# A transformer block with cross attention: residual rows, layer norm statistics and stores moved, and one more pair of softmax units transposed on the vector engine

## The chip, the cores and the metric

One core of a Trainium2 chip runs the kernel. The core has a matrix engine (TensorE, PE in the profile, with its weight loads as PEld), a vector engine (VectorE, DVE), an activation engine (ScalarE, ACT), a general engine (GpSimd, POOL) and a sync engine (SyncE, SP) that here only issues transfers. Each engine works through its own instructions in order, and waits on semaphores for what other engines or transfers still owe it. Transfers (DMA) can be issued by SP, ACT or POOL; an instruction that issues one and has to wait holds up everything behind it on that engine.

The metric is the time of one execution in microseconds. The runs before had a median of 835.01 us (834.54 to 835.21). The profile comes from one further execution.

## What is computed

Four batches (B = 4) of 512 rows of width 512, all in float32. With `x` the rows and `c` the context rows of a batch, the reference is, cut to what matters:

```
h   = layer_norm(x, ln1_w, ln1_b)
q   = heads(h @ q_w + q_b);  k = heads(c @ k_w + k_b);  v = heads(c @ v_w + v_b)     # 16 heads of 32
a   = softmax(q k^T / sqrt(32) + mask) v
hid = a @ cproj_w + cproj_b + x
y   = gelu(layer_norm(hid, ln2_w, ln2_b) @ fc_w + fc_b) @ proj_w + proj_b            # inner width 2048
out = hid + y
```

## The kernel before

**Tiling.** The program is a straight line of instructions that Python loops write out. The 16 heads of a batch are handled in four groups of four; a group of a batch is `w` (0 to 15, batch = w // 4). The 512 query rows of a group go in four *units* of 128 rows; unit `u = 4 w + qt` counts from 0 to 63. Two neighbouring units are a *pair*, `2 w + half`, 0 to 31.

**A unit** (`scores`, L227). TensorE makes the scores of four heads into a PSUM tile `sc`, of which there is only one, so the next unit's scores wait until VectorE has read it. VectorE adds the mask and takes the row minimum of the negated scores (L239, four instructions); ScalarE makes the exponentials and their sums (L243, four).

**Turning a unit** (`turn`, L247). The probabilities have to be transposed before they meet `v`. In most pairs VectorE transposes 32 by 32 blocks into a tile `tb` (L271, four per unit; after the second unit also the reciprocal sums, L276 to L279), and 16 transfers of 136 KB, issued by SP, exchange the blocks between the partition groups (`copies`, L299). There are two `tb` tiles, so pair p + 2 (or the next one after it to use them) waits for the exchange of pair p. The exchange writes to a tile `pT`, of which there is one, or, for the pairs in `IN_G`, to `gt`, a tile that the MLP needs only later; the pairs in `IN_XE` use `xe` at the end. `exchange` (L288) keeps back a pair bound for `pT` until the pair before it in `pT` has been attended. The pairs in `ON_PE` are instead transposed on TensorE (L257, 16 small matrix instructions a unit into PSUM), copied out by VectorE and ScalarE (L260, L262), and their sums transposed on TensorE as well (`turn_sums`, L326).

**Attending a pair** (`attend`, L336): TensorE multiplies by `v` (L356), VectorE scales the result into `oT` (L361). It comes ahead of the scores of a later unit; by default pair p is attended at unit 2 p + 4, and the table `AT` sets other units.

**Work between the units.** The lists `first[w]` and `later[w]` (L757 to L827) hold what is put between the units of a group: projections to k, q and v of a group two or more ahead (`prep_k`, `prep_q`, `prep_v`), layer norm 1 of a later batch (`inputs`: loads of x into four `xn` tiles, statistics, normalisation, transposes on TensorE with eviction by VectorE and ScalarE), the projection `cproj` of a finished batch (`C`), layer norm 2, and the pieces of the MLP of batches 0 and 1 (`fc`, `proj`). Each piece has a cost (3.4 for a chain of matrix work, 0.5 for a transpose step, 0 for loads and vector work); the loop at L830 hands pieces out so that each half of a unit gets its share of the list's cost. So a piece's place in the list sets its place on every engine's queue.

**Loads.** `Q[0]` issues most loads: POOL in batch 0 (w = 0 to 3), SP from w = 4 on (L833). `load_w` loads a group's weights, `load_mlp` keeps up to eight tiles of MLP weights ahead, `load_hid` loads residual rows into `hid` and adds a bias row to them on POOL (`add_row`, L368). For batch 0 the residual rows are x itself; for the later batches `cproj` adds x and the bias (tiles `ct`), stores the sum to a DRAM tile `xa` (L401), and `load_yn` and `load_hid` read it back.

**cproj and layer norm 2** (L389, L414). `cproj` of row tile t is one chain of TensorE, then VectorE adds it to `hid` (batch 0) or `ct` (L397). In batches 0 and 3 VectorE takes the statistics of the sum at once (`ln_stat`, two instructions). `ln_rs` makes the reciprocal deviations on POOL, `norm2` normalises on VectorE, `ln2_turn` transposes on TensorE into `yT`.

**The end.** The MLPs of batches 2 and 3 run after the attention (`last_mlps`, L513), with a scheme of seven products in place of eight. It works in pairs of inner tiles (`fc_pair`), and VectorE makes the sums that it needs, of the weights (`sum_wa`), of `yT` (`y_sums`) and of the results.

Of the kernel before, what the change touches and what calls it, by code (L numbers as in the profile page):

```python
# [40 lines left out]
P = 128  # L44
B, L, D, H = 4, 512, 512, 16
HD = D // H
INNER = 4 * D
NT = L // P
# [8 lines left out]
AHEAD = 3  # L57
NORMAL = 2
LAG = 4
IN_G = (2, 5, 7)  # L60
IN_XE = (29, 31)
AT = {7: 1, 9: 2, 13: 4, 15: 5}
ON_PE = (0, 3)
MW = 8
WARM = 14
PW = 2 * NT * HG * HD
# [7 lines left out]
def xattn_block(ctx: ExitStack, tc: tile.TileContext, x, encT, mask, q_w, k_w, v_w, c_w, fc_w, p_w, vecs, rows, out):  # L74
# [29 lines left out]
    S = {}  # L104
# [6 lines left out]
    def ln_stat(key, t, src):  # L111
        if t == 0:
            S["mv", key] = small.tile([P, NT, 2], F32, tag="mv", name=f"mv{key[0]}_{key[1]}")
        st = small.tile([P, 6], F32, tag="st", name=f"st{key[0]}_{key[1]}_{t}")
        nc.vector.bn_stats(st, src)
        nc.vector.bn_aggr(S["mv", key][:, t, :], st)
# [63 lines left out]
    def load_w(w, queue=None, names=("wk", "wq", "wv")):  # L180

        if w >= NW:
            return
        g = w % NG
        for n, src in (("wk", k_w), ("wq", q_w), ("wv", v_w)):
            if n in names:
                S[n, w] = (two if n == "wk" else one).tile([P, ND, P], F32, tag=n, name=f"{n}_{w}")
                (queue or Q[0]).dma_start(out=S[n, w], in_=src[:, g, :, :])
# [21 lines left out]
    def prep_v(w):  # L210
        b = w // NG
        v = five.tile([P, NT, P], F32, tag="v", name=f"v_{w}")
        acc = acc_tile(f"accv_{w}")
        for t in range(NT):
            for d in range(ND):
                nc.tensor.matmul(  # L216
                    acc[:, ts(t, P)], eT[:, d, ts(t, P)], S["wv", w][:, d, :],
                    start=(d == 0), stop=(d == ND - 1),
                )
        load_w(w + 1, names=("wv",))  # L220
        nc.scalar.copy(v, acc.rearrange("p (t f) -> p t f", t=NT))  # L221
        bias = row[:, 2, ts(w % NG, P)]
        nc.gpsimd.tensor_tensor(v, v, bias[:, None, :].broadcast_to([P, NT, P]), ALU.add)  # L223
        S["v", w] = v
# [151 lines left out]
        for t in ts_:  # L376
            add_row(S["hid", b, t], 1 if b else 0)

    def load_ct(b, t):

        if t == 0:
            S["xa", b] = dram.tile([L, D], F32, tag=f"xa{b}", name=f"xa{b}")
        if b == B - 1:
            S["ct", b, t] = tiles.tile([P, D], F32, tag="xn", name=f"ct_{b}_{t}")
        else:
            S["ct", b, t] = two.tile([P, D], F32, tag="ct", name=f"ct_{b}_{t}")
        Q[0].dma_start(out=S["ct", b, t], in_=x[b, ts(t, P), :])

    def cproj(b, t):  # L389
        h = S["hid", b, t] if b == 0 else S["ct", b, t]  # L390
        if b:
            for i in range(NT if b == B - 1 else 2) if t == 0 else (t,) if t > 1 and b < B - 1 else ():
                add_row(S["ct", b, i], 0)
        acc = acc_tile(f"accc_{b}_{t}")
        for g in range(NG):
            nc.tensor.matmul(acc, S["oT", b][:, g, ts(t, P)], wc[:, g, :], start=(g == 0), stop=(g == NG - 1))  # L396
        nc.vector.tensor_tensor(h, acc, h, ALU.add)  # L397
        if b in (0, B - 1):
            ln_stat((2, b), t, h)
        if b:  # L400
            nc.sync.dma_start(out=S["xa", b][ts(t, P), :], in_=h)  # L401
            if t + 2 < NT and b < B - 1:
                load_ct(b, t + 2)

    def load_yn(b):

# [2 lines left out]
            Q[0].dma_start(out=S["yn", b][t], in_=S["xa", b][ts(t, P), :])  # L409

    def stat2(b, t):
        ln_stat((2, b), t, S["yn", b][t])

    def norm2(b, t):  # L414
        if b == 0 and t == 0:
            S["yn", b] = [tiles.tile([P, D], F32, tag="xn", name=f"xn2_{b}_{i}") for i in range(NT)]
        if b == B - 1 and t == 0:
            S["yn", b] = [S["ct", b, i] for i in range(NT)]
        ln_norm((2, b), t, S["yn", b][t], S["yn", b][t] if b else S["hid", b, t])
# [42 lines left out]
    def proj(b, q, t):  # L462
        acc = acc_tile(f"accp_{b}_{q}_{t}")
        for k in range(FQ):
            nc.tensor.matmul(  # L465
                acc, gT[q % 2][:, k, ts(t, P)], S["pw", b, q * FQ + k], start=(k == 0), stop=(k == FQ - 1)
            )
        h = S["hid", b, t]
        nc.vector.tensor_tensor(h, acc, h, ALU.add)  # L469
        if q == NQ - 1:  # L470
            nc.sync.dma_start(out=out[b, ts(t, P), :], in_=h)
        count[1] += 1
        load_mlp()

# [38 lines left out]
    def last_mlps():  # L513
# [137 lines left out]
        for b in range(NORMAL, B):  # L651
            for c in range(NP):
                if b == NORMAL:
                    for i in range(2):
                        nc.sync.dma_start(out=pb[:, c, i, :], in_=p_w[ts(2 * c + i, P), :])
                fc_pair(b, c, lambda: sum_wa(c + 1) if c + 1 < NP else None)
                if c + 2 < NP:
                    load_wa(c + 2)
                elif b + 1 < B:
                    load_wa(c + 2 - NP)  # L660
                if c % 2 == 0 and c:
                    g_sums(c - 2)
                if b + 1 < B and 1 <= c <= NT:
                    norm2(b + 1, c - 1)
            g_sums(NP - 2)

            def sums(b=b):
                if b == NORMAL:
                    for c in range(0, NP, 2):
                        p_sums(c)  # L670
                if b + 1 < B:
                    load_hid(b + 1, range(NT))

            def turns(b=b):
                if b + 1 < B:
                    run(turns2(b + 1))

            def middle(b=b):
                if b + 1 < B:
                    y_sums(b + 1)  # L680
                    sum_wa(0)

            project(b, sums, turns, middle)
# [5 lines left out]
    def do(fn):  # L689
        return [(0.0, fn)]  # L690
# [69 lines left out]
    load2, k2, q2, v2 = A(2)  # L760
    load3, k3, q3, v3 = A(3)
    load4, k4, q4, v4 = A(4)
    first[0] = do(lambda: load_w(2, names=("wk",))) + [(CHAIN, lambda: prep_v(1)), (CHAIN, lambda: prep_q(1))] + x1 + [load2, k2, q2]
    first[1] = x2[:1] + [v2, load3, k3] + x2[1:2] + [q3] + x2[2:] + [v3] + x4 + x3
    first[2] = do(load_mlp) + [load4, q4, k4, v4] + A(5)[:2]
    first[3] = A(5)[2:] + A(6)
    mlp = []
    for p in range(NORMAL):
# [6 lines left out]
    def hid_(b, *ts_):  # L775
        return do(lambda: load_hid(b, ts_))
# [7 lines left out]
    def rs(b):  # L784
        return do(lambda: ln_rs((2, b)))
# [6 lines left out]


    x1, x2, x3, x4 = inputs(2)
    first[3] += x1
    load, k, q, v = A(7)
    c, t2 = C(0), turns2(0)
    first[4] = [load, k] + x2[:2] + [q] + x2[2:] + [v] + x3[:2] + x4 + hid_(0, 0, 1, 2, 3)
    later[4] = c[:1] + x3[2:] + c[1:] + rs(0)
    load, k, q, v = A(8)  # L800
    first[5] = norm(0, 0, 1) + [load, q] + norm(0, 2, 3) + [k] + t2 + [v] + do(lambda: proj_bias(0)) + some(5)
    load, k, q, v = A(9)
    x1, x2, x3, x4 = inputs(3)
    first[6] = [load, k, q] + some(5) + [v] + x1
# [65 lines left out]
    load_wa(1)  # L870
    sum_wa(0)
    run(C(B - 1))
    ln_rs((2, B - 1))
    load_hid(NORMAL, range(NT))
    att.close()
    last_mlps()
# [44 lines left out]
```

## Time and profile before

| what | value |
|---|---|
| median of the runs | 835.01 us |
| profiled execution, its own time | 838.42 us |
| span in that execution | 836.6 us |
| TensorE busy | 812.7 us, 4064 matrix instructions |
| VectorE busy | 557.9 us |
| ScalarE busy | 342.3 us |
| GpSimd busy | 109.5 us |
| transfers | 136.87 MB, mean 164 GB/s |

How to read the profile. The busy part of the page gives each engine's time; a row of digits shows it in 40 slices of the span, in tenths, and PEclk is the clock that TensorE was granted, in tenths of full speed. A line of a timeline has start, duration, engine, line of the kernel, operation, the tiles written and read, the shape and a count; where the engine sat idle before it, square brackets hold the idle time and what ended it. SPq and POOL lines with DMA_DIRECT2D are issues of transfers. A line of waits has the engine and line that waited, whom for, the total, the number of times and the longest. A line of the table by stages has the stretch, its length, and then each engine's busy time with its number of instructions (PE, PEld, DVE, ACT, POOL), the granted clock, the share of the transfer engines and GB/s. A piece of the chain has start, duration and what ran. A matrix instruction of the program is two in the profile, so x32 in a row of `av` is one attended pair.

### The profile page before, as it was taken

What the parts mean: (1) busy time and instruction counts of PE and PEld (TensorE: products, weight loads), DVE (VectorE), ACT (ScalarE), POOL (GpSimd) and SP (SyncE); (2) the same over time, 40 slices, a digit from 0 to 9 for tenths busy, and PEclk for the clock granted to TensorE, in tenths of its full rate; (3) what the DMA queues carried; (4) which work ended last, traced back from release to release, by engine and by line L of the source; (5) the groups of instructions that cost most, each with busy time, mean ns of one, the idle gap of its engine ahead of it and who ended that gap; (6) DMA issues with size and microseconds to landing.
All of it is one profiled execution on the core that took longest, in us unless ns stands there. A gap on an engine that the chain in (4) does not pass through costs nothing.

```text
span 836.6 us, 11984 instructions
## 1 busy us (share of the span) xinstructions
PE 812.7 (97%) x4064; PEld 472.9 (57%) x4064; DVE 557.9 (67%) x1259; ACT 342.3 (41%) x740; POOL 109.5 (13%) x132
## 2 busy tenths in 40 slices
PE   9998999979999999999999999999999999999998
PEld 6545545434445554453554435444446888888887
DVE  3596988478666785876887486877337987268511
ACT  2555654316765553455544357455200431023200
POOL 2313312023000021000100210000013003200011
PEclk9998999989999999999999999999999999999999
DMA  5465798828777777687777776985835550022001
GB/s 205 157 154 158 231 236 223 204 75 197 185 184 209 208 202 217 172 211 186 211 202 194 222 200 166 247 196 126 247 108 182 160 193 34 15 87 76 12 13 38
DMA packets 59164, 136.87 MB, mean 164 GB/s; under 512 B 12144, under 2 KB 14320, under 8 KB 58976
## 3 DMA queue, kind: packets, MB, share of 16 engines
q1 hardware_dynamic: 55056, 122.99, 54.5%
q0 software_dynamic: 3520, 12.00, 4.5%
q10 hardware_dynamic: 528, 1.14, 0.6%
q8 instruction: 32, 0.52, 0.3%
q14 instruction: 28, 0.23, 0.1%
HBM read 61.89 MB, written 7.34 MB: 83 GB/s over the span
## 4 chain that ended last, share of the span: by engine, by line
PE 82%; DVE 7%; DMA 4%; SPq 3%; POOL 1%; issue 1%; ACT 0%; DVEq 0%; ACTq 0%; POOLq 0%
PE accp L465 13%; PE accf L455 12%; PE q L559 12%; PE sc L234 7%; PE av L356 6%; PE accv L216 5%; PE accq L204 5%; PE acck L195 5%; PE accc L396 3%; DVE s L239 2%; SPq L313 2%; DVE tb L271 2%; DMA xn<-x_dram 2%; PE q4p L599 2%; PE q3p L599 2%; PE q5p L599 2%
## 5 line engine op out<-in xcount | busy, mean ns | idle before, releaser
L243 ACT ACTIVATE s<-s,mn 128x512 f32<-128x512 f32 x256 | 181.6, 710 | 181.5 <-DVE mn L239 181.2
L239 DVE CUSTOM_DVE_ANT_0 s<-sc,mb 128x512 f32<-128x512 f32 x256 | 161.2, 686 | 47.9 <-PE sc L234 47.8
L271 DVE STREAM_TRANSPOSE tb<-s 128x512 f32<-128x512 f32 x240 | 152.6, 684 | 6.1 <-ACT s L243 5.0
L455 PE MATMUL accf<-yT,fcw 128*128 128x512 f32 x256 | 114.9, 599 | 0.0
L465 PE MATMUL accp<-pw,gt 128*128 128x512 f32 x256 | 114.3, 598 | 0.0
L455 PEld LDWEIGHTS accf<-yT,fcw 128*128 128x128 f32 x256 | 47.1, 190 | 65.0 <-issue 61.0
L465 PEld LDWEIGHTS accp<-pw,gt 128*128 128x128 f32 x256 | 47.4, 190 | 63.2 <-issue 60.5
L234 PE MATMUL sc<-kT,qT 32*128 32x512 f32 x512 | 73.6, 645 | 2.2 <-DVE mn L239 1.4
L396 PE MATMUL accc<-wc,oT 128*128 128x512 f32 x128 | 59.2, 614 | 6.7 <-DVE hid L397 6.7
L216 PEld LDWEIGHTS accv<-wv,xe 128*128 128x128 f32 x512 | 58.9, 192 | 9.4 <-issue 8.4
L559 PE MATMUL q<-ys,gt 128*128 128x256 f32 x256 | 60.3, 380 | 0.7 <-issue 0.7
L216 PE MATMUL accv<-wv,xe 128*128 128x128 f32 x512 | 60.6, 277 | 0.0
L195 PE MATMUL acck<-xe,wk 128*128 128x512 f32 x128 | 58.7, 601 | 0.0
L204 PE MATMUL accq<-xe,wq 128*128 128x512 f32 x128 | 58.5, 599 | 0.0
L356 PE MATMUL av<-pT,v 128*32 128x256 f32 x864 | 53.9, 391 | 4.5 <-DMA pT<-tb 3.2
L559 PEld LDWEIGHTS q<-ys,gt 128*128 128x128 f32 x256 | 48.5, 190 | 7.9 <-issue 1.0
L469 DVE TENSOR_TENSOR hid<-accp,hid 128x512 f32<-128x512 f32 x32 | 21.9, 684 | 40.2 <-PE accp L465 40.1
L243 ACT ACTIVATION_READ_ACCUMULATOR s<-s,mn 128x1 f32 x256 | 47.7, 187 | 0.0
L223 POOL TENSOR_TENSOR v<-v,row 128x512 f32<-128x512 f32 x16 | 20.4, 1276 | 203.4 <-ACT v L221 203.2
L396 PEld LDWEIGHTS accc<-wc,oT 128*128 128x128 f32 x128 | 24.4, 196 | 39.5 <-issue 31.0
L559 PE MATMUL q<-yT,gt 128*128 128x256 f32 x192 | 46.3, 379 | 0.0
L356 PEld LDWEIGHTS av<-pT,v 128*32 128x32 f32 x864 | 26.5, 112 | 33.9 <-issue 18.7
(122 smaller groups left out, 875.6 us busy)
## 6 DMA issues: line engine op xcount, KB each, us to landing
pT<-tb SPq DMA_DIRECT2D x400, 136.0 KB, 2.4
pw<-p_w_dram SPq DMA_DIRECT2D x32, 256.0 KB, 4.0
gt<-fc_w_dram SPq DMA_DIRECT2D x32, 256.0 KB, 2.9
gt<-tb SPq DMA_DIRECT2D x48, 136.0 KB, 3.8
fcw<-fc_w_dram SPq DMA_DIRECT2D x24, 256.0 KB, 3.3
pb<-p_w_dram SPq DMA_DIRECT2D x16, 256.0 KB, 3.7
xe<-tb SPq DMA_DIRECT2D x24, 136.0 KB, 2.4
xe<-encT_dram SPq DMA_DIRECT2D x12, 256.0 KB, 3.8
```

What stands on the lines that cost most here:

```text
L195: nc.tensor.matmul(acc, S["wk", w][:, d, :], eT[:, d, :], start=(d == 0), stop=(d == ND - 1))
L204: nc.tensor.matmul(acc, S["wq", w][:, d, :], xT[:, d, :], start=(d == 0), stop=(d == ND - 1))
L216: nc.tensor.matmul(acc[:, ts(t, P)], eT[:, d, ts(t, P)], S["wv", w][:, d, :], start=(d == 0), stop=(d == ND - 1),)
L234: nc.tensor.matmul(sc[:, h, :], qT[r, ts(qt, P)], kT[r, :], start=True, stop=True)
L239: nc.vector.tensor_tensor_reduce(out=s, in0=sc[:, h, :], in1=S["mb", w // NG], scale=1.0, scalar=FMAX, op0=ALU.add, op1=ALU.min, accum_out=mn,
L243: nc.scalar.activation(s, s, AF.Exp, bias=mn, scale=-1.0, accum_out=sums[:, qt, h : h + 1])
L271: nc.vector.transpose(tv[:, q, h], S["ps", w, qt][h])
L356: nc.tensor.matmul(av[ts(h, HD), : 2 * P].rearrange(shape, **kw), v[:, t, ts(h, HD)], p[t][h], start=(t == 0), stop=(t == NT - 1),)
L396: nc.tensor.matmul(acc, S["oT", b][:, g, ts(t, P)], wc[:, g, :], start=(g == 0), stop=(g == NG - 1))
L455: nc.tensor.matmul(acc, S["fcw", b, f][:, d, :], S["yT", b][:, d, :], start=(d == 0), stop=(d == ND - 1))
L465: nc.tensor.matmul(acc, gT[q % 2][:, k, ts(t, P)], S["pw", b, q * FQ + k], start=(k == 0), stop=(k == FQ - 1))
L559: nc.tensor.matmul(o, a[:, k], y[:, k], start=(k == 0), stop=(k == 1))
```

## The change

- `IN_G` becomes (2, 4, 6) and `ON_PE` becomes (0,). Pair 3 is now turned by VectorE and exchanged like the others. The pairs of batch 0 from 1 on use `pT` and `gt` by turns.
- `AT` attends pair 3 at unit 11 (10 before) and pair 6 at unit 17 (16 before).
- The first eight MLP weight tiles are loaded at the end of `first[0]` instead of the start of `first[2]`, in both places by POOL.
- The residual rows of batch 0 are loaded at the end of `first[3]`, ahead of x for batch 2, by POOL, where they were at the end of `first[4]`, by SP. Their row additions on POOL move along.
- Batch 0's statistics for layer norm 2 leave `cproj` and stand in `first[5]`, after unit 20's scores; its normalisation follows, and its transposes come after v's projection instead of before.
- Batch 3's statistics leave `cproj` and stand between the inner pairs 0, 1 and 3 of batch 2's last MLP; its normalisation moves from pairs 1 to 4 to pairs 4, 5 and 7.
- In batches 1 and 2 the stores to `xa` and the loads of `ct` for t = 2 and 3 are issued by POOL instead of SP; so are the four output stores of batch 0.

```diff
-IN_G = (2, 5, 7)
+IN_G = (2, 4, 6)
-AT = {7: 1, 9: 2, 13: 4, 15: 5}
-ON_PE = (0, 3)
+AT = {7: 1, 9: 2, 11: 3, 13: 4, 15: 5, 17: 6}
+ON_PE = (0,)
...
-    def load_ct(b, t):
+    def load_ct(b, t, queue=None):
...
-        Q[0].dma_start(out=S["ct", b, t], in_=x[b, ts(t, P), :])
+        (queue or Q[0]).dma_start(out=S["ct", b, t], in_=x[b, ts(t, P), :])
...
         nc.vector.tensor_tensor(h, acc, h, ALU.add)
-        if b in (0, B - 1):
-            ln_stat((2, b), t, h)
         if b:
-            nc.sync.dma_start(out=S["xa", b][ts(t, P), :], in_=h)
+            (nc.sync if b == B - 1 else nc.gpsimd).dma_start(out=S["xa", b][ts(t, P), :], in_=h)
             if t + 2 < NT and b < B - 1:
-                load_ct(b, t + 2)
+                load_ct(b, t + 2, nc.gpsimd)
...
-        ln_stat((2, b), t, S["yn", b][t])
+        ln_stat((2, b), t, S["hid", b, t] if b == 0 else S["ct", b, t] if b == B - 1 else S["yn", b][t])
...
-            nc.sync.dma_start(out=out[b, ts(t, P), :], in_=h)
+            (nc.gpsimd if b == 0 else nc.sync).dma_start(out=out[b, ts(t, P), :], in_=h)
...
-                if b + 1 < B and 1 <= c <= NT:
-                    norm2(b + 1, c - 1)
+
+                if b + 1 < B:
+                    for t in {0: (0,), 1: (1, 2), 3: (3,)}.get(c, ()):
+                        stat2(b + 1, t)
+                    if c == 3:
+                        ln_rs((2, b + 1))
+                    for t in {4: (0,), 5: (1, 2), 7: (3,)}.get(c, ()):
+                        norm2(b + 1, t)
...
-    first[0] = do(lambda: load_w(2, names=("wk",))) + [(CHAIN, lambda: prep_v(1)), (CHAIN, lambda: prep_q(1))] + x1 + [load2, k2, q2]
+    first[0] = do(lambda: load_w(2, names=("wk",))) + [(CHAIN, lambda: prep_v(1)), (CHAIN, lambda: prep_q(1))] + x1 + [load2, k2, q2] + do(load_mlp)
...
-    first[2] = do(load_mlp) + [load4, q4, k4, v4] + A(5)[:2]
+    first[2] = [load4, q4, k4, v4] + A(5)[:2]
...
-    first[3] += x1
+    first[3] += hid_(0, 0, 1, 2, 3) + x1
...
-    first[4] = [load, k] + x2[:2] + [q] + x2[2:] + [v] + x3[:2] + x4 + hid_(0, 0, 1, 2, 3)
-    later[4] = c[:1] + x3[2:] + c[1:] + rs(0)
+    first[4] = [load, k] + x2[:2] + [q] + x2[2:] + [v] + x3[:2] + x4
+    later[4] = c[:1] + x3[2:] + c[1:]
...
-    first[5] = norm(0, 0, 1) + [load, q] + norm(0, 2, 3) + [k] + t2 + [v] + do(lambda: proj_bias(0)) + some(5)
+    first[5] = stat(0, 0, 1) + [load, q] + stat(0, 2, 3) + rs(0) + [k] + norm(0, 0, 1, 2, 3) + [v]
+    first[5] += t2 + do(lambda: proj_bias(0)) + some(5)
...
     run(C(B - 1))
-    ln_rs((2, B - 1))
```

## The prediction

> **What bounds the kernel now.** I read the page's engine shares first, then TensorE's waits, then the timelines of the places that these waits name.
>
> ```profile
> PE 812.7 (97%) x4064; PEld 472.9 (57%) x4064; DVE 557.9 (67%) x1259; ACT 342.3 (41%) x740; POOL 109.5 (13%) x132
> PEclk9998999989999999999999999999999999999999
> ```
>
> TensorE has 812.7 of 836.6 us, so an edit is worth what it takes out of TensorE's work, of its idle stretches, or of the two slices with a lower clock. Its waits, and where they lie:
>
> ```profile
> PE accc L396 <- DVE hid L397: 6.7, 1, 6.7
> PE av L356 <- DMA pT<-tb: 3.2, 2, 1.7
> PE tp L136 <- DVE xn L127: 1.7, 1, 1.7
> PE tpp L257 <- ACT s L243: 1.6, 1, 1.6
> ...
> 65.72 2.16 PE L257 MATMUL tpp<-ident,s 128*128 128x128 f32 x12 [1.60 <-ACT s L243]
> ...
> 172.88 5.63 PE L396 MATMUL accc<-wc,oT 128*128 128x512 f32 x8 [6.70 <-DVE hid L397]
> ...
> 498.69 1.93 PE L356 MATMUL av<-pT,v 128*32 128x256 f32 x32 [1.67 <-DMA pT<-tb]
> ```
>
> Nearly all of it stands before 200 us; 498.69 is in batch 2. VectorE is the second bound there:
>
> ```profile
> 49.13:135.80 86.67, 81.18 (x566) 45.77 (x562) 71.93 (x179) 46.59 (x116) 22.25 (x35) 0.96 0.77 207
> ```
>
> Units 4 to 16 hold 81.2 us of TensorE and 71.9 of VectorE. Last, the queues around the long wait:
>
> ```profile
> 132.74 0.55 POOL L188 DMA_DIRECT2D wv<-v_w_dram  x1 [6.15 <-PE accv L216]
> 133.30 1.28 POOL L223 TENSOR_TENSOR v<-v,row 128x512 f32<-128x512 f32 x1
> 134.51 2.21 POOL L154 DMA_DIRECT2D xn<-x_dram  x4
> ...
> 135.29 13.09 SPq L313 DMA_DIRECT2D gt<-tb  x16
> ...
> 166.36 1.85 SPq L375 DMA_DIRECT2D hid<-x_dram  x4
> ...
> 170.84 4.93 POOL L368 TENSOR_TENSOR hid<-hid,row 128x512 f32<-128x512 f32 x4 [19.96 <-DMA hid<-x_dram]
> ```
>
> The rows of x for the first residual (hid) are issued at 166.36, behind pair 8's 16 exchange transfers on SP; VectorE and TensorE wait for them.
>
> **Pair 3 leaves TensorE.** Two unit transposes at 1.75 us (the chain's piece at 29.52) and the sums' 0.31 go: 3.8 us of TensorE, with its waits of 1.60 and 0.53 for unit 6's exponentials. VectorE gains eight tb transposes (24.2 us for 40, so 0.61 each) and one of 0.45, and loses four copies of 0.69: +2.5. Then VectorE needs 74.4 us in this stage, and TensorE 81.2 - 3.8 - 2.9 (what the half-clock stretch at 67 to 74 us cost: av 3.57 for 1.86, the scores after it 1.72 for 1.07, the rest in tpp) = 74.5. Neither covers the other any more, so I walk it. Pair 3's exchange costs SP 16 x 0.64 = 10.2 us and lands about 2.4 later; its turn ends near 78, SP is free from about 75, attend(3) comes near 95: hidden.
>
> The eight fc loads (2.1 MB) move from 83 us to right behind the wq load at 47.42 on POOL, 8 x 0.55 = 4.4 us, in front of the next weight load at 54.34, so nothing queues. But they meet pair 1's exchange, which SP issues from 49.6 and which landed at 63.9 (my reading of the transfers' own landings); 2.1 MB at 353 GB/s (79 to 95 us moved 247 GB/s at a transfer share of 0.70) is 6 us of transfer, of which 2 to 3 fit ahead of the exchange. I put the landing at 67 (bounds 64 to 70). attend(1), freed of the transposes, wants it at 64.1: a wait of 3 takes the place of 2.1. The projection of q behind layer norm 1's transposes then waits for VectorE, which reaches those evictions at 78.4 to 80, against 83.1 before. From there my walk stays 3.3 to 5 us ahead to unit 13: **g = 4.0**. Attend(6), behind two projections now, loses its wait for the exchange: **+1.5**.
>
> On the clock the Trainium skill ("TensorE: Matmul & The Clock Gate", What's actually happening) says that it halves after an idle window of some 3.4 us. This trace dropped it after 1.6 us of idle with transposes around it, and did not after 1.67 us at 497. By the page my 3 us wait at 64 costs nothing more, by the row up to 2.9; g lies between.
>
> **hid moves to the end of w = 3, ahead of x for batch 2.** It takes away the 6.70, the half-clock that followed (5.63 for 3.6: 2.0), and VectorE's backlog from it: 0.48 before scores, 1.67 and three of 0.13 in layer norm 2's transposes. **+11.2.** But on POOL these are four loads (2.2 us) and then four row additions (1.27 each), which wait for the landings, and only then the four xn loads. Before, xn was issued at 134.51 to 136.18 beside an exchange and landed 3.0 to 8.2 us later:
>
> ```profile
> 136.18 8.20 DMA xn<-x_dram
> ```
>
> Let E be the end of v's projection of w = 6 (132.44 before). hid takes xn's old place: it lands at E+5 to E+12, the fourth addition ends at E+13.2, the xn loads go out at E+13.2 to E+15.4, at the tail of pair 7's exchange and beside three weight loads. With 4 to 5 us each the last lands at E+19.5 (bounds: without collision in hid E+16.5; with another 8.2, E+23). VectorE stands at its statistics, before unit 17's minima; then 0.85 + 0.42 + 2.46 + 0.46 until the first transpose: E+23.7. TensorE reaches it at E + 1.07 + 3.6 + 3.63 + 1.86 + 1.07 + 3.67 = E+14.9. **-8.8**, nothing else being queued ahead of it, and a half clock behind it: none to 2.2, I take **-1.1**.
>
> **Layer norm 2 of batch 0.** Statistics (4 x 0.8) now stand behind unit 20's minima, and the transposes directly ahead of fc(0), with v's projection before them, no longer between. From scores(20) to fc(0) VectorE has 2.5 minima, 3.3 statistics, 2.4 tb, 1.8 norm, 2.5 minima, 0.7 eviction, 2.4 tb, 0.95 sums, 0.7 eviction = 17.3; TensorE has 7.2 + 1.1 + 3.6 + 1.8 = 13.7. **-3.6** (cover gone; before, the 3.6 of v hid the evictions).
>
> Up to fc(0): 4.0 + 1.5 + 11.2 - 8.8 - 1.1 - 3.6 = +3.2. After it TensorE is bound again, VectorE with slack.
>
> **xa stores, ct loads and batch 0's outputs to POOL.** In batch 2:
>
> ```profile
> 473.85 0.53 SPq L401 DMA_DIRECT2D xa<-ct  x1
> 476.36 0.34 SPq L387 DMA_DIRECT2D ct<-x_dram  x1
> ...
> 481.74 4.59 SPq L401 DMA_DIRECT2D xa<-ct  x2
> 486.47 10.25 SPq L313 DMA_DIRECT2D pT<-tb  x16
> ```
>
> The first store waits for SP, and the last store's wait for VectorE holds the next exchange from 485.4 to 486.47. On POOL, 12 issues of 0.55 per two batches besides waits; queued behind are ct's additions (about 0.8 us earlier than before by my walk) and v's, which have a unit's slack. The exchange goes out 1.0 to 1.9 us earlier and the waits of 1.67 and 0.29 (scores at 488.82) end: **+1.7** (0.5 to 2.0). Batch 1 has 0.2 to win.
>
> Against it stands a rule of the skill ("SBUF — State Buffer", A bandwidth-pool intuition that's wrong): a transfer issued by POOL can be starved by VectorE's two-port operations, 3.1 us for 0.62. The POOL rows above took 0.55 with VectorE over 85% busy, so I cost an issue at 0.55.
>
> **Batch 3's statistics.**
>
> ```profile
> 639.12 0.69 DVE L487 TENSOR_TENSOR ys<-yT,ys 128x512 f32<-128x512 f32 x1
> ...
> 639.91 3.69 PE L559 MATMUL q<-ys,gt 128*128 128x256 f32 x16 [0.67 <-issue]
> ```
>
> Without the 0.87 of statistics ahead of them the ys sums end before TensorE asks: **+0.7**. The 3.4 us go into a stage with 42.8 of 46 us busy on VectorE, but its results are read a pair (5.8 us) later, and at most 1.7 comes at once: hidden.
>
> **Sum.** 3.2 + 1.7 + 0.2 + 0.7 = 5.8. The profiled execution took 838.42 with a span of 836.6; its span falls to about 830.8. The median of the runs, 835.01, is 3.4 below that execution; I take the difference off it: 829.2. A change under 0.2% (1.7 us) can't be told from none.
>
> **Rivals.**
> - *hid's landings don't collide* (0.22): xn at E+16.5 and no half clock: 3 + 1.1 more, 825. For it: hid before landed in 4.4 to 4.9. Against: pair 7's exchange is on SP in just those microseconds.
> - *The front gains nothing* (0.14): pair 1 lands at 70 with a half clock behind (g = 2) and xn comes at E+22: -4.5, some 833.8. That the front part doesn't do what it is for is this case.
> - *POOL is starved* (0.07), the slower end: if the issues of hid and xn behind v(6) take the page's 3.1 us, 8 x 2.55 = 20 us later xn, about 849. It decides from 5.8 + 1.7 = 7.5 us of delay, 1.5 us an issue.
> - The sum as it stands (0.57): 826.5 to 832.5.
>
> Range: from 823.5 (first rival with 1.5 below) to 835 (second with 1.2 above). Faster: 0.57 + 0.22 and a third of the second, 0.83; same 0.09; slower 0.08.
>
> **What would show it.** In the trace after: no tpp in unit 6, and av for pair 1 waiting 0 to 6 us for its exchange; no wait of accc for hid; instead layer norm 1's second set of transposes waiting 6 to 12 us for xn; fc(0) waiting 2 to 5 us on an eviction; no wait for an exchange at 490 to 500; ys without wait. I am wrong if xn lands before E+15, if VectorE's stage from unit 4 to 16 takes over 83 us, or if POOL's issues grow.

## The result, and the profile after

The changed kernel is slower. Its median is 841.15 us (839.38 to 845.05), beside 835.72 us (834.54 to 839.2) of the kernel before on the same chip, six runs each (those of before include the three whose median is 835.01): 5.4 us between the medians. The ratio on record, which is not the quotient of the medians (1.0065), is 1.0055, 95% interval 1.0031 to 1.0078, about 4.6 us. In a second comparison, on the chip of several of the experiments below, it was 840.42 against 837.19: ratio 1.0032 (1.0017 to 1.0047), 2.7 us. The forecast was 829.2 with a range of 823.5 to 835. The profiled execution took 841.57 us with a span of 839.8, beside 838.42 and 836.6 before.

Engine shares and granted clock of the page after:

```profile
PE 809.9 (96%) x4030; PEld 469.5 (56%) x4030; DVE 557.1 (66%) x1264; ACT 339.9 (40%) x735; POOL 119.8 (14%) x152
PEclk9998899699999999999999999999999999999999
```

TensorE is busy 2.8 us less, as pair 3's transposes are gone, and yet the span is 3.2 longer. The clock row shows why to look ahead of 170 us: slices of 8, 8 and 6 tenths, where before there were two of 8. TensorE's waits after:

```profile
PE tp L137 <- ACT s L244: 10.2, 1, 10.2
PE av L357 <- DMA gt<-tb: 8.9, 2, 5.7
PE sc L235 <- DVE mn L240: 2.4, 2, 1.8
PE av L357 <- ACT gt L455: 1.7, 1, 1.7
...
PE tp L137 <- ACT v L222: 0.9, 1, 0.9
...
PE accf L454 <- DVE yT L140: 0.4, 1, 0.4
```

The wait for hid (6.70) is gone, as are the waits in unit 6's transposes. In their place stand one wait of 10.17 and two of 5.66 and 3.20. TensorE's timeline gives their places:

```profile
68.59 3.64 PE L357 MATMUL av<-pT,v 128*32 128x256 f32 x32 [5.66 <-DMA gt<-tb]
...
99.00 3.64 PE L357 MATMUL av<-pT,v 128*32 128x256 f32 x32 [3.20 <-DMA gt<-tb]
...
159.59 2.60 PE L137 MATMUL tp<-ident,xn 128*128 128x128 f32 x8 [10.17 <-ACT s L244]
162.12 3.64 PE L357 MATMUL av<-pT,v 128*32 128x256 f32 x32
...
493.30 1.14 PE L235 MATMUL sc<-kT,qT 32*128 32x512 f32 x8 [1.80 <-DVE mn L240]
...
643.62 3.62 PE L558 MATMUL q<-ys,gt 128*128 128x256 f32 x16
```

The first two are waits for the exchanges of pair 1 and pair 3. The profile names the transfer that ended last, here one of the next pair (`gt`); by their own landings pair 1's last transfer came at 68.21 and pair 3's at 98.65. The third is for the normalized rows of batch 2, whose last load lands at 155.30 (below); the profile names the last engine of the chain from there. The fourth is for batch 2's row 2. An attended pair takes 1.93 us at full clock and 3.64 behind each of the first three waits: the granted clock was half there. The last line is the `ys` product of batch 3, which now waits for nothing. The issues of transfers that explain the first three, on SP and on POOL:

```profile
46.76 4.31 POOL L446 DMA_DIRECT2D fcw<-fc_w_dram  x8
...
48.47 15.26 SPq L314 DMA_DIRECT2D pT<-tb  x16
...
80.80 13.97 SPq L314 DMA_DIRECT2D pT<-tb  x16
...
136.64 2.21 POOL L376 DMA_DIRECT2D hid<-x_dram  x4
139.63 2.67 POOL L369 TENSOR_TENSOR hid<-hid,row 128x512 f32<-128x512 f32 x2 [0.78 <-DMA hid<-x_dram]
143.27 1.28 POOL L369 TENSOR_TENSOR hid<-hid,row 128x512 f32<-128x512 f32 x1 [0.96 <-DMA hid<-x_dram]
145.41 1.27 POOL L369 TENSOR_TENSOR hid<-hid,row 128x512 f32<-128x512 f32 x1 [0.87 <-DMA hid<-x_dram]
146.63 2.18 POOL L155 DMA_DIRECT2D xn<-x_dram  x4
```

The eight fc loads go out just ahead of pair 1's exchange, whose 16 issues then take 15.26 us instead of the 10.47 of before. Pair 3's take 13.97. The rows of x for batch 2 (`xn`) go out only at 146.63, when the fourth addition to hid is done; their last transfer runs in the chain of work from 148.26 to 155.30:

```profile
148.26 7.04 DMA xn<-x_dram
```

Where the time went is read from the start of each unit's scores, in the kernel's profile less in that of before, with the difference at unit 0 taken off (microseconds; minus is sooner). The last column is the end of the span. The labels are those of the experiments below.

| kernel | unit 15 | unit 22 | unit 52 | unit 54 | end |
|---|---|---|---|---|---|
| after | +3.33 | +4.44 | +4.17 | +5.74 | +4.35 |
| forecast for it | -4.0 | -3.2 | -3.4 | -5.1 | -5.8 |
| after, second profile | +2.63 | +3.81 | +3.54 | +6.57 | +5.18 |
| e1_stores_sp | -0.88 | +0.83 | +0.56 | -0.14 | -1.52 |
| e3_x_first | +0.09 | -2.58 | -2.85 | +1.15 | -0.24 |
| e2_pair3_pe | -0.38 | +1.98 | +1.71 | +0.26 | -1.14 |
| e4b_fc_late | -4.49 | -1.81 | -2.08 | -0.17 | -1.55 |
| e12_hid_behind | +1.78 | -8.52 | -8.59 | -4.29 | -5.44 |
| e10_hid_early | -4.69 | -14.38 | -14.65 | -16.08 | -16.79 |
| e9_b_front | +3.65 | -8.58 | -7.31 | -9.14 | -9.16 |
| e11_front_fc_late | -4.50 | -13.43 | -12.62 | -12.99 | -13.01 |
| e5_b_hid_early | -2.24 | -13.54 | -13.50 | -13.59 | -13.59 |
| e6_b_stats3 | -2.44 | +0.56 | +0.80 | -0.51 | -1.65 |
| e8_b_stores_pool | -2.18 | -0.43 | -0.70 | -2.09 | -2.24 |
| v1 | -4.61 | -15.75 | -16.02 | -17.00 | -18.15 |
| v2_pool | -4.23 | -15.96 | -16.23 | -17.73 | -19.11 |

Against the forecast 7.3 us are missing by unit 15, and 3.3 more between units 52 and 54. The stretch between 15 and 22, with the longest wait of all, came out as summed (1.1 lost, 0.8 forecast).

One profiled execution is not the kernel, though. Up to unit 15 five of these executions run the same program as the changed kernel (its own two, e1, e3 and e12), and they stand at +3.33, +2.63, -0.88, +0.09 and +1.78. All five wait 5.6 to 8.5 us for pair 1; what sets them apart is in good part whether the wait for pair 3 (2.17 to 3.20 us) is followed by half clock, as in the first two, or not. So by unit 15 the miss is 3.1 to 7.3 us. Of the old order (before, e5, e6, e8) the same column has 0, -2.24, -2.44 and -2.18.

### The profile page after: what moved, and what is told of

Read it like the earlier page. It is cut to its first block, busy times and chain, and to the rows that moved or that the text cites. A ratio compares the mean times of both kernels' runs of the same rounds, so it can differ in the third digit from the quotient of the medians.

```text
span 839.8 us, 11953 instructions
## 1 busy us (share of the span) xinstructions
PE 809.9 (96%) x4030; PEld 469.5 (56%) x4030; DVE 557.1 (66%) x1264; ACT 339.9 (40%) x735; POOL 119.8 (14%) x152
## 3 DMA queue, kind: packets, MB, share of 16 engines
q10 hardware_dynamic: 528, 1.14, 0.6%
## 4 chain that ended last, share of the span: by engine, by line
PE 85%; DMA 7%; DVE 3%; ACT 2%; POOL 1%; issue 1%; SPq 1%; DVEq 0%; POOLq 0%; ACTq 0%
PE accp L464 13%; PE accf L454 12%; PE q L558 12%; PE sc L235 7%; PE av L357 7%; PE accv L217 6%; PE acck L196 5%; PE accc L397 5%; PE accq L205 5%; DMA pT<-tb 3%; PE tp L137 2%; PE q4p L598 2%; PE q3p L598 2%; PE q5p L598 2%; PE q6p L598 2%; PE q1p L598 2%
## 5 line engine op out<-in xcount | busy, mean ns | idle before, releaser
L272 DVE STREAM_TRANSPOSE tb<-s 128x512 f32<-128x512 f32 x248 | 157.6, 683 | 12.1 <-DMA gt<-tb 6.8
L357 PE MATMUL av<-pT,v 128*32 128x256 f32 x864 | 57.3, 410 | 10.6 <-DMA gt<-tb 8.9
L397 PE MATMUL accc<-wc,oT 128*128 128x512 f32 x128 | 57.0, 597 | 0.0
L235 PEld LDWEIGHTS sc<-kT,qT 32*128 32x128 f32 x512 | 20.6, 188 | 39.1 <-issue 20.4
```

Of the source, the lines that this page charges most:

```text
L235: nc.tensor.matmul(sc[:, h, :], qT[r, ts(qt, P)], kT[r, :], start=True, stop=True)
L272: nc.vector.transpose(tv[:, q, h], S["ps", w, qt][h])
L357: nc.tensor.matmul(av[ts(h, HD), : 2 * P].rearrange(shape, **kw), v[:, t, ts(h, HD)], p[t][h], start=(t == 0), stop=(t == NT - 1),)
```

## The experiments

Every comparison is against the kernel before, run beside it on the same chip (four chips, with medians of before of 837.36, 837.19, 836.92 and 836.59 us). Theory at the start: the front lost its gain to the fc loads, which meet pair 1's exchange, and batch 2 its gain to the order on POOL. Rival: the loss belongs to pair 3, whose exchange was costed at nothing.

**Undoing one part of the changed kernel.** First its stores, back on SP (statistics, rows of hid and everything else as changed):

```diff
-            (nc.sync if b == B - 1 else nc.gpsimd).dma_start(out=S["xa", b]...)
+            nc.sync.dma_start(out=S["xa", b]...)
...
-                load_ct(b, t + 2, nc.gpsimd)
+                load_ct(b, t + 2)
...
-            (nc.gpsimd if b == 0 else nc.sync).dma_start(out=out[b, ...])
+            nc.sync.dma_start(out=out[b, ...])
```

> The changed kernel with one part undone: xa stores, the later ct loads and batch 0's outputs are issued by SP again. Theory (POOL's order costs time in batch 2: the addition of ct_2 stands behind the issue of ct_3's load, which waits for the landing of a store): the waits at units 53 and 54, 1.80 and 1.74 us in the changed kernel, return to the 0.29 and 1.67 of before, 1.5 us faster than the changed kernel, some 839.7 us against its 841.2. Rival (the stores' place does not matter, the wait at 53 comes from the front part's shift): same time as the changed kernel within 0.5 us, and the two waits stay.

Measured: 837.12, ratio 1.0003 (0.9982 to 1.0024). In its profile units 52 to 54 gain 0.7 where the changed kernel lost 1.6: 2.3 us, where the theory had 1.5. But unit 15 was also 4.2 us sooner than in the changed kernel's profile, where this edit does nothing: the wait for pair 3's exchange was 2.17 in this execution, not 3.20, and no half clock followed. By the ratios the edit is worth 2.4 to 4.4 us; its own stretch accounts for 2.3.

Then pair 3, back on TensorE, with its attends and exchanges (fc loads stay early, attend(6) late):

```diff
-IN_G = (2, 4, 6)
...
-AT = {7: 1, 9: 2, 11: 3, 13: 4, 15: 5, 17: 6}
-ON_PE = (0,)
+IN_G = (2, 5, 7)
...
+AT = {7: 1, 9: 2, 13: 4, 15: 5, 17: 6}
+ON_PE = (0, 3)
```

> The changed kernel with pair 3 transposed on TensorE again (pair 6 still attended at unit 17, all else as changed). Theory (the seventh exchange is what the front can't hold: it runs beside the context loads, lands 18 us after its start, and TensorE waits 3.20 us and then runs at half clock): unit 11's scores come where they were before, within 1 us, instead of 3.6 us later, with no wait for an exchange at pair 3; pair 1's wait of 5.66 shrinks below 2 because the transposes of unit 6 lie in it; all in all 2.5 to 4 us faster than the changed kernel, 837 to 838.7. Rival (pair 1's collision with the fc loads is what costs, pair 3 only takes its place): less than 1 us faster, the wait for pair 1 stays above 4.

Measured: 836.4, ratio 0.9998 (0.9985 to 1.0011), 0.6 us below the theory's band, and by the ratios 2.8 to 4.8 us below the changed kernel; unit 12 starts within 0.4 us of before. Pair 1's exchange is stretched here too:

```profile
49.08 15.93 SPq L314 DMA_DIRECT2D pT<-tb  x16
...
70.88 1.93 PE L357 MATMUL av<-pT,v 128*32 128x256 f32 x32 [2.39 <-ACT pT L263]
```

but the pair waits 2.39 us and not 5.66, since pair 3's transposes stand ahead of it, and full clock follows. (The copy that the line names writes into the `tb` tile that pair 1's exchange frees at 70.2.) So the early fc loads cost less while that cover is there, none against the profile of before and some 2 us at unit 15 against the executions of the old order without its half clock (e5, e6): most of the loss comes from the two edits together.

Now the fc loads alone, put to the front of `first[5]`, behind pair 9's exchange:

```diff
-    first[0] = ... + [load2, k2, q2] + do(load_mlp)
+    first[0] = ... + [load2, k2, q2]
...
-    first[5] = stat(0, 0, 1) + [load, q] + ...
+    first[5] = do(load_mlp) + stat(0, 0, 1) + [load, q] + ...
```

> The changed kernel with the first eight fc loads issued only at the start of w = 5, by SP, so that they meet neither pair 1's nor pair 3's exchange. Theory (the collision costs pair 1's wait): attend(1) waits under 2 us instead of 5.66 and no half clock follows, so unit 8 comes 4 us earlier; pair 3's wait stays between 1 and 3 us since the context loads still collide with it; fc(0) then waits for its weights not at all or up to 2 us, and 3 to 5 us are left: 836 to 838. Rival (VectorE bound the stage from unit 4 to 16 anyway, 74.4 us of work): unit 13 comes less than 2 us earlier than in the changed kernel.

Measured: 835.47, ratio 0.9964 (0.9948 to 0.998), 0.5 us below its band and by the ratios 5.7 to 7.6 us below the changed kernel. Pair 1's 16 issues take 10.47 us again:

```profile
48.83 10.47 SPq L314 DMA_DIRECT2D pT<-tb  x16
```

and TensorE's waits for exchanges shrink from 8.9 to 1.4:

```profile
PE tp L137 <- ACT s L244: 11.8, 1, 11.8
...
PE av L357 <- DMA gt<-tb: 1.4, 1, 1.4
```

Unit 15 is 4.5 sooner than before, against the forecast's 4.0. The wait for the normalized rows is 11.8: with the front in time, it only grows. Pair 3's exchange is still slow without the fc loads: 12.73 us of issues, beside the context rows and weights that POOL loads then, and it lands at 93.94 with that wait of 1.44.

**The order of hid and xn.** Batch 2's rows ahead of hid's, both still on POOL:

```diff
-    first[3] += hid_(0, 0, 1, 2, 3) + x1
+    first[3] += x1 + hid_(0, 0, 1, 2, 3)
```

> The changed kernel with the loads of x for batch 2 ahead of hid's loads and additions on POOL, nothing else. Theory (the 10.2 us wait of layer norm 1's transposes is xn behind hid's additions): the wait falls to 2 to 3 us (now the reciprocal deviations stand behind the additions on POOL), the half clock behind it goes, the scores of unit 18 come 9 to 13 us earlier, and of that 7 to 10 us are left at the end: 831 to 834. Rival (VectorE is the bound of that stretch and takes the time back before fc(0)): under 4 us faster, with new waits for VectorE between units 19 and 22.

Measured: 836.49, ratio 0.9989 (0.9968 to 1.001), 2.5 us above the theory's band. The wait fell to 6.3, not to 2 to 3. The theory had named the cause, that GpSimd also computes the rows' reciprocal deviations (rstd, `rs`) and now does so behind the four additions, but had it too small: the additions wait for hid's landings, 6.9 to 10.3 us after their issue here:

```profile
134.41 2.21 POOL L155 DMA_DIRECT2D xn<-x_dram  x4
136.61 2.16 POOL L376 DMA_DIRECT2D hid<-x_dram  x4
...
148.62 1.26 POOL L369 TENSOR_TENSOR hid<-hid,row 128x512 f32<-128x512 f32 x1 [0.49 <-DMA hid<-x_dram]
...
150.74 1.03 POOL L124 TENSOR_TENSOR rs<-ve,nhalf 128x4 f32<-128x4 f32 x1
```

So hid has to come behind the rows *and* their statistics. In the next two kernels its loads stand behind the first two transposed rows, ahead of pair 8's exchange on SP: later than in the changed kernel, sooner than before. The first has the fc loads late as well:

```diff
-    first[3] += hid_(0, 0, 1, 2, 3) + x1
-    first[4] = [load, k] + x2[:2] + [q] + ...
+    first[3] += x1
+    first[4] = [load, k] + x2[:2] + hid_(0, 0, 1, 2, 3) + [q] + ...
```

> The changed kernel with two edits: the fc loads late (as in the run before of that name) and batch 0's rows into hid loaded two transposed rows earlier; its second normalization stays where the change put it, and so do the stores on GpSimd. Theory: the 10 to 12 us wait for the normalized rows is hid's lateness alone, so it shrinks below 2 us; 819 to 824. Rival: the place of the statistics and of rstd on GpSimd costs by itself: 4 us or more of that wait stay; 827 to 831.

> The changed kernel with one edit: the four loads of hid stand behind the first two transposed rows of batch 2's x, as in e10_hid_early; the fc loads stay early. Theory: the wait for the normalized rows (10.2 us and the half clock behind it) goes and the fc loads' cost stays: 11 us below the changed kernel, 828 to 831. Rival: with the front late, the rows come in time anyway or another load takes their place: less than 6 us below the changed kernel, 834 or more.

Measured: with late fc loads 822.61, ratio 0.9831 (0.9801 to 0.9862); with this edit alone 830.75, ratio 0.9912 (0.9874 to 0.9949). The first text's "hid's lateness" is put wrongly (the changed kernel has hid earlier than this one), but its number holds: the wait is gone. Its rival, that the new place of the statistics costs 4 us or more by itself, falls. GpSimd of the first:

```profile
129.04 2.21 POOL L155 DMA_DIRECT2D xn<-x_dram  x4
...
138.69 1.03 POOL L124 TENSOR_TENSOR rs<-ve,nhalf 128x4 f32<-128x4 f32 x1
148.02 4.96 POOL L369 TENSOR_TENSOR hid<-hid,row 128x512 f32<-128x512 f32 x4 [8.30 <-DMA hid<-x_dram]
```

The rows' loads go out right behind the bias addition to v of w = 6, rstd is done at 139.7, and the additions to hid still end at 153, in time for the output projection. The four kernels make a square, in ratios to before:

| | hid ahead of xn (as changed) | hid behind |
|---|---|---|
| fc loads early (as changed) | 1.0032 and 1.0055 | 0.9912 |
| fc loads late | 0.9964 | 0.9831 |

Late fc loads are worth 5.7 to 7.6 us in the left column and 6.8 in the right; hid behind xn is worth 10 to 12 and 11. Within their intervals the two costs are separate and add up.

**Doing one part alone, on the kernel before.** First hid alone:

```diff
-    first[4] = [load, k] + x2[:2] + [q] + x2[2:] + [v] + x3[:2] + x4 + hid_(0, 0, 1, 2, 3)
+    first[4] = [load, k] + x2[:2] + hid_(0, 0, 1, 2, 3) + [q] + x2[2:] + [v] + x3[:2] + x4
```

> The kernel before with one edit: the four loads of batch 0's rows into hid stand two transposed rows earlier, ahead of pair 8's exchange on the SP queue. Theory: the wait for hid at the output projection (6.7 us) and the half clock behind it go, 8.7 to 11.2 us faster than before; 824 to 828. Rival: the projections only reach the next late operand (the row additions on GpSimd, or pair 8's exchange pushed back by 1 MB of loads), less than 4 us faster; 831 to 835.

Measured: 823.68, ratio 0.9841 (0.9802 to 0.988), 13 us for one moved term. Units 15 to 22 gain 11.3, as the prediction's +11.2 says; the 2.2 us that stand at unit 15 already are not the edit's doing, but this execution had full clock where that of before had half.

Then the new order of pairs alone, and the same with late fc loads:

```diff
-IN_G = (2, 5, 7)
...
-AT = {7: 1, 9: 2, 13: 4, 15: 5}
-ON_PE = (0, 3)
+IN_G = (2, 4, 6)
...
+AT = {7: 1, 9: 2, 11: 3, 13: 4, 15: 5, 17: 6}
+ON_PE = (0,)
```

```diff
-    first[2] = do(load_mlp) + [load4, ...]
+    first[2] = [load4, ...]
...
-    first[5] = norm(0, 0, 1) + ...
+    first[5] = do(load_mlp) + norm(0, 0, 1) + ...
```

> The kernel before with the first batch's order alone: pair 3 no longer transposed on TensorE, the exchanges and attends moved as in the changed kernel; the fc loads, batch 0's second normalization, the statistics and all stores stay. Theory (the prediction's g without the collision): 4 to 4.5 us earlier at unit 15, and carried to the end, since the loads of hid move up with the walk; 831 to 832.5. Rival: the gain is given back at the output projection's wait for hid, which grows from 6.7 to about 10 us; 834.5 to 836.

> The kernel before with the first batch's order of pairs (as in e9_b_front) and the fc loads moved behind pair 9's exchange; the loads of hid stand where they stood in the code. Theory: the order of exchanges alone puts hid ahead of pair 8's exchange, and nothing else needs moving: the 9.2 us wait of e9_b_front goes and the gain at the output projection stays; 820 to 824. Rival: that gain was there only because the wait of 9.2 us gave hid time: the front is 8 us earlier, and a wait for hid of 5 us or more stands at the output projection again; 827 to 831.

Measured: 831.31, ratio 0.9937 (0.9913 to 0.9961), and 824.8, ratio 0.9866 (0.9842 to 0.989), the second 0.8 us above its band. The first hits its number for the wrong reasons. Its fc loads stand where they stood, near 80 us, and now meet pair 3's exchange:

```profile
100.94 3.64 PE L356 MATMUL av<-pT,v 128*32 128x256 f32 x32 [9.23 <-DMA gt<-tb]
...
76.78 15.67 SPq L313 DMA_DIRECT2D pT<-tb  x16
...
78.20 3.23 POOL L447 DMA_DIRECT2D fcw<-fc_w_dram  x6
...
154.36 2.36 SPq L375 DMA_DIRECT2D hid<-x_dram  x4
157.54 11.83 SPq L313 DMA_DIRECT2D pT<-tb  x16
```

A wait of 9.23 us eats the front. But pair 7 is now bound for `pT`, so `exchange` keeps pair 8 back until pair 7 has been attended at unit 18 (153.85 here); before, pair 7 went to `gt`, and pair 8 was let go at unit 17, at 152.88. So SP reaches hid *ahead* of pair 8's exchange, 12 us sooner than before, and the wait for hid is gone. The second run refutes the rival that the front's delay had given hid its time: with the front 8 us sooner there is still no wait for hid, whose loads go out at 146.31. So the new order of exchanges removes the 6.70 by itself, and hid's move to POOL brought only the wait for xn.

Last the two small parts, each alone: the stores of batches 1 and 2 and their next rows on POOL, and batch 3's statistics:

```diff
-            nc.sync.dma_start(out=S["xa", b]...)
+            (nc.sync if b == B - 1 else nc.gpsimd).dma_start(out=S["xa", b]...)
...
-                load_ct(b, t + 2)
+                load_ct(b, t + 2, nc.gpsimd)
```

> The kernel before with one edit: the attended rows of batches 1 and 2 are stored, and their next rows loaded, on the POOL queue as in the changed kernel. The prediction's term: 1.7 us faster (0.5 to 2.0). Theory from the changed kernel's trace: each load waits for the store ahead of it, which lands only 4 to 5 us after its issue, and row 2's addition stands behind the issue of row 3's load on GpSimd; 0.5 to 2.5 us slower, with a wait of VectorE for the row of about 6 us in batch 2.

```diff
-        if b in (0, B - 1):
+        if b == 0:
...
-                if b + 1 < B and 1 <= c <= NT:
-                    norm2(b + 1, c - 1)
+                if b + 1 < B:
+                    for t in {0: (0,), 1: (1, 2), 3: (3,)}.get(c, ()):
+                        stat2(b + 1, t)
...
-    ln_rs((2, B - 1))
```

> The kernel before with the last batch's statistics alone moved from the output projection's rows to the place between the pair sums. The prediction's term: the wait of 0.67 us for ys goes, 0.7 us faster. Rival: the statistics now stand between VectorE's evictions and cost as much there; no change.

Measured: stores 835.51, ratio 0.9983 (0.9971 to 0.9996); statistics 835.61, ratio 0.9985 (0.9973 to 0.9997). By the ratios they gain 1.4 and 1.3 us, barely clear of none. The theory that the stores on POOL always cost time falls: the same edit lost in some executions and not in others. That it gains is not shown either: between units 52 and 54 this execution gains 1.4, but the seven with these stores on SP spread from 0 (before) to 1.8 (e9) there. The changed kernel's batch 2, on GpSimd, VectorE and SP, shows how it lost:

```profile
473.99 0.56 POOL L400 DMA_DIRECT2D xa<-ct  x1
478.37 0.54 POOL L388 DMA_DIRECT2D ct<-x_dram  x1 [3.83 <-DMA xa<-ct]
478.90 0.54 POOL L400 DMA_DIRECT2D xa<-ct  x1
484.03 0.54 POOL L388 DMA_DIRECT2D ct<-x_dram  x1 [4.60 <-DMA xa<-ct]
484.59 1.28 POOL L369 TENSOR_TENSOR ct<-ct,row 128x512 f32<-128x512 f32 x1
...
485.90 0.69 DVE L398 TENSOR_TENSOR ct<-accc,ct 128x512 f32<-128x512 f32 x1 [6.95 <-POOL ct L369]
...
490.82 9.62 SPq L314 DMA_DIRECT2D pT<-tb  x15
```

and GpSimd where the edit is alone:

```profile
468.71 0.60 POOL L401 DMA_DIRECT2D xa<-ct  x1
472.36 0.54 POOL L387 DMA_DIRECT2D ct<-x_dram  x1 [3.04 <-DMA xa<-ct]
...
476.99 0.54 POOL L387 DMA_DIRECT2D ct<-x_dram  x1 [3.56 <-DMA xa<-ct]
477.55 1.29 POOL L368 TENSOR_TENSOR ct<-ct,row 128x512 f32<-128x512 f32 x1
```

On one queue each load waits for the store that frees its buffer, and row 2's addition stands behind the load of row 3: it starts 3.1 us after row 2 landed (481.50) in the first, 1.5 (476.03) in the second; before it was 0.2. Where the two stores land 4.1 to 4.4 and 4.8 or more after issue, units 52 to 54 lose 1.6 to 4.3 (five profiles); where they take 3.1 to 3.8, these units gain 1.4 to 1.5 (four). Issued by SP, the same two stores took 2.5 to 2.7 and 3.0 to 4.4 us. What sets the landing is not settled: in both cases an exchange is being issued at that time.

**The version that beats both.** The changed kernel with fc loads late, hid behind the first transposed rows, batch 0's second normalization as before and all stores on SP; and the same with the stores of batches 1 and 2 on POOL. Against the changed kernel, without the lines of the stores and statistics shown above:

```diff
-    first[0] = ... + [load2, k2, q2] + do(load_mlp)
+    first[0] = ... + [load2, k2, q2]
-    first[3] += hid_(0, 0, 1, 2, 3) + x1
-    first[4] = [load, k] + x2[:2] + [q] + ...
-    later[4] = c[:1] + x3[2:] + c[1:]
+    first[3] += x1
+    first[4] = [load, k] + x2[:2] + hid_(0, 0, 1, 2, 3) + [q] + ...
+    later[4] = c[:1] + x3[2:] + c[1:] + rs(0)
-    first[5] = stat(0, 0, 1) + [load, q] + stat(0, 2, 3) + rs(0) + [k] + norm(0, 0, 1, 2, 3) + [v]
-    first[5] += t2 + ...
+    first[5] = do(load_mlp) + norm(0, 0, 1) + [load, q] + norm(0, 2, 3) + [k] + t2 + [v] + ...
```

> The changed kernel with four of its parts undone: the fc loads go back behind the first pairs (to just before the second normalization of batch 0), batch 0's rows into hid are loaded two transposed rows earlier and ahead of pair 8's exchange, its second normalization runs as it did before (statistics behind each row of the output projection, normalized before unit 16), all stores on the SP queue. Pair 3 stays exchanged by transfer and attend(1) to attend(6) stay late. Theory: the front keeps the 4.5 us that the run with late fc loads had at unit 15, the 6.7 us wait for hid with its half clock and backlog (11.2 us) goes and no 10 us wait for the normalized rows comes; 819 to 825. Rival: the wait moves to another operand (pair 8's exchange or the fc loads behind it) and less than half of that is left; 828 to 833.

> The fastest kernel so far (fc loads late, hid early, the old place of batch 0's normalization) with the attended rows of batches 1 and 2 stored, and their next rows loaded, on the POOL queue. As that edit alone did to the kernel before: 1.4 us faster, about 819. If the landings are late as in the changed kernel's own trace (4 to 5 us a store): 1.5 to 3 us slower, 822 to 823.5, with VectorE waiting 6 to 7 us for row 2 in batch 2.

Measured: 820.57, ratio 0.9801 (0.9769 to 0.9834), and 820.76, ratio 0.9814 (0.9783 to 0.9846): 16 us below before, the queue of the stores making no difference that shows. The first gains 1.4 us more than e10 between units 15 and 22, where they differ in the place of batch 0's second normalization. Its longest waits of TensorE are these:

```profile
PE tp L137 <- ACT v L222: 2.4, 1, 2.4
PE av L357 <- DMA hid<-x_dram: 1.9, 1, 1.9
```

## Why the prediction was wrong

The sum was +3.2 up to fc(0), +1.7, +0.2 and +0.7. By its steps:

**"g = 4.0" failed**, and by more than all the rest: it came out as -3.3 by unit 15 in the profile, and between +0.9 and -3.3 in the five executions. Three of its terms are at fault. *The landing of pair 1*: "at 67 (bounds 64 to 70)". It landed at 68.21 in a profile that ran 1.2 ahead, so near the upper bound, and the wait was 5.66 for 3. The term took "353 GB/s" for the transfers; with the transfer engines at a share of 1.03 to 1.04 they moved 243 to 264 (94 to 108 us here, 90 to 106 in e9). *"attend(3) comes near 95: hidden"*: this step was taken at SP's 10.2 us from a free queue at 78, and put at nothing. SP began at 80.80 and needed 13.97; the exchange landed at 98.65, with a wait of 3.20, and even without the fc loads it was not hidden (1.44). *The clock*: in this profile both waits halved it (0.79 granted in 62 to 78 us, 0.76 in 94 to 108), where the prediction had left that open inside g. Behind pair 3 the half clock alone cost 2.7 us (13.96 us from attend(3) to attend(4), 11.26 in e1), and whether it came was luck, as three of the five executions were spared. Without the fc loads ahead of it, g is right: 4.5.

**What the distance to the median held.** Of the 12.0 us between 841.15 and 829.2, 9.0 lie in the profiled executions (839.8 for a span of 830.8). The other 3.0 come from the last step, which took off the 3.4 us by which the profile of before stood above its median; the changed kernel's stands 0.4 above its own, and on the four chips of the experiments the medians of before are only 1.1 to 1.8 below 838.42. g held 2.9 us for the half-clock stretch at 67 to 74 us of that execution, so part may have been counted twice. The tables by stage, before and in the run with batch 3's statistics alone, whose front is the same program:

```profile
62.00:78.00 16.00, 13.77 (x90) 7.70 (x90) 10.65 (x29) 6.71 (x18) 1.80 (x3) 0.79 0.67 167
...
62.00:78.00 16.00, 13.68 (x119) 9.92 (x118) 11.70 (x32) 9.56 (x23) 4.25 (x7) 1.00 0.66 173
```

With full clock, or a shorter dip (e8), the old front reaches unit 15 from 2.2 to 2.4 us sooner than in the execution that the sum was worked from. Against those the new order is worth some 2.2 us, not 4. That the median of before had this gain at its end is not shown: e6 and e8 lost theirs again by unit 22 (+0.56 and -0.43), to another half-clock stretch at 190 to 210 us (0.87 and 0.93 granted) that the execution before did not have.

**hid and xn were right**: "+11.2" measured as 11.3 alone (e5), "-8.8" as 10.17, and the last row landed at E+20.7 for E+19.5, E being 134.57. The half clock behind it cost about 2.5 us for 1.1 (the transposes, the attended pair and the scores against those of e12). What the prediction did not see is that the 11.2 were to be had without the 8.8: it costed hid's move as the edit that frees it, while the new order of exchanges, by holding pair 8 back, did so by itself.

**"-3.6" for layer norm 2** was too much: the waits ahead of fc(0) are 0.93 and 0.38. This and the half clock cancel, so that the stretch fits is luck.

**Batch 2's "+1.7" failed in this kernel**, by 3.3 us; alone 1.4 was measured, which is within what the same stretch varies by. The prediction named ct's additions as queued behind POOL's issues and gave them slack by a walk in which stores land as fast as on SP (2.5 us); at 4.1 and 4.85 the slack is gone.

**Batch 3's "+0.7" was right in kind** and too small: the `ys` wait ended, and from unit 54 to the end 1.4 us were gained here and 1.1 in e6.

**The rivals.** The nearest is "The front gains nothing": pair 1 landed as it said, with the half clock, but at its g = 2 it was still too kind, since it too took pair 3's exchange as hidden. "POOL is starved" did not occur: the issues shown from POOL took 0.54 to 0.60 us each. No rival held a second exchange that comes late; the slower side came from that and from batch 2, not from GpSimd.

## What to carry to other kernels

In these runs a chain of small exchange transfers was as long as the traffic beside it let it be (10.1 to 16.7 us of issues): before an edit puts work behind one, list every load that is issued in its time, also those that the same edit moves there. When two edits aim at one wait, ask whether the first already removes it; here the new order of exchanges did, and the second only put four additions ahead of the next rows and their rstd. And before a half-clock stretch of one profiled execution is booked as a gain of the edit, look at further executions of the same stretch: here they differed by 2.4 us with the old front and by 4.2 with the new one.

## What was unexpected in the hardware

Pair 1's exchange of 2.2 MB beside 2.1 MB of loads took 15.3 to 16.7 us of issues (six executions), and 10.1 to 10.5 without them (ten); in the changed kernel it landed 19.7 us after its first issue, before 14.3. The loads waited as well: they landed 7 to 15 us after issue in e9, against 3.0 to 5.7 where the last exchange had just been issued (e4b).

The clock does not follow the length of a wait alone. Waits of 2.41 (v1) and 2.59 (the changed kernel's second profile) were followed by half clock, waits of 2.17 (e1) and 2.54 (e12) at the same kind of place by full clock, and a wait of 1.60 in unit 6 by either (half in e8, full in e5). The granted clock in the traces shows more. Its half-clock stretches last 3.41 us or two to four times that, and within an execution they begin whole multiples of 3.413 us apart: in the changed kernel at 67.15, 97.87 and 152.48, which is 9 and 16 steps. I laid such a grid over each of the fifteen profiles that have half clock before 560 us. From 20 us to there, each of the 27 steps at full clock in which TensorE idled 2.07 us or more was followed by half clock, none with less than 1.65 was, and of the ten between, four were. So the place of a wait on the grid matters. Here are the steps around the wait for pair 3, first in the changed kernel (3.20 us, of which 2.07 in one step), then in e12 (2.54 us, cut into 0.97 and 1.58):

```profile
94.46:97.87 3.41, 1.34 (x12) 1.15 (x11) 1.19 (x4) 2.85 (x9) 1.03 (x2) 1.00 1.06 250
97.87:104.70 6.83, 5.70 (x41) 2.24 (x41) 2.92 (x5) 0.00 (x0) 1.29 (x2) 0.50 1.02 239
...
95.62:99.03 3.41, 2.44 (x22) 2.25 (x21) 2.29 (x8) 2.86 (x9) 0.55 (x1) 1.00 0.99 235
99.03:102.44 3.41, 1.83 (x32) 1.13 (x32) 1.50 (x3) 0.54 (x2) 1.77 (x2) 1.00 0.94 258
```

An idle window of some 3.4 us, as the Trainium skill gives it in "TensorE: Matmul & The Clock Gate" (What's actually happening), is thus no safe lower bound here: 2.07 us within one step were enough. Every wait of 5.6 us and more, and that of 3.20, came with 6.8 to 13.7 us at half clock.
